# A four-layer graph network on one core: the last dense layer with features on partitions, and rooms given by what older graphs still need

## The chip, the core and the metric

The kernel runs on one core of a Trainium2 chip. Its time is the device time of one execution in microseconds (us). Before the change, three timed runs gave 2318.75, 2318.81 and 2318.9 us; the median is 2318.81.

## What is computed

There are 32 independent graphs of 512 nodes with 256 features each, and four layers; `x` is a graph's features (512 x 256) and `adj` its weights (512 x 512), all in float32. Cut to what matters, with biases kept:

```python
def L0(x):  h = (1 + eps) * x + adj @ x;      return relu(h @ W1 + b1) @ W2 + b2
def L1(x):  h = adj @ (x @ W.T + b);          return where(h > 0, h, alpha * h)
def L2(x):  h = layer_norm(x, gamma, beta)
            return x + relu((adj @ h) @ W_rel + b_rel + h @ W_root)
def L3(x):  h = (eps * x + adj @ x) @ W1 + b1               # 256 -> 1024
            h = silu(h * rsqrt(mean(h * h) + 1e-6) * w)
            return h @ W2 + b2                              # 1024 -> 256
for L in (L0, L1, L2, L3):
    x = layernorm(x + L(x))
```

The change concerns the last line of L3, `h @ W2 + b2`, and the sum with `x` that follows it.

## The kernel before

**Tiles and stages.** A graph's features are kept "by token": token 4p + c is on partition p, in chunk c, so that a tile is 128 x (4 chunks x 256 features). Between the layers' steps they are also kept with features on partitions: `aT` or `hT`, 128 x 512 tokens for each chunk of 128 features. A large product is made of seven products of blocks instead of eight (`seven`, line 651): blocks of both sides are added and subtracted beforehand (`left_sums`, `right_sums`, `weight_sums`), and the results are put together from PSUM with `take` (first write to a block) and `put` (a later one). A graph passes through `layer0`, `layer1`, `layer2`, `layer3` (lines 1046 to 1137). Each calls `aggregate` (line 767: adj @ x, 14 matmuls of 256 columns) and then its dense steps.

**Layer 3.** `layer3` (line 1100) aggregates, adds the row b2 to `x` (`plus_row`, line 1019: two additions of 128 x 512), makes the 1024 hidden features with features on partitions (`dense_feat`, line 807, into `hT`), sums their squares, takes the mean's power -1/2 through a DRAM line back to all partitions (`everywhere`, line 997: a store of `few` into `line`, then a load of `line` into a room), multiplies and applies silu, forms `right` from blocks of hidden features (`dense_sums`), and then makes the second dense layer in `dense_add` (line 850). There a block of hidden features, 128 x 128, is the stationary operand and a block of W2, 128 columns, is moved: the result is by token, and each of the seven products is added straight into `x` by VectorE. When both halves of a token half are there, `norm.half` sums the features and squares of that half for the layer norm; `norm.scaled` writes the result, and one DMA stores the graph.

**Turning.** Layer 2 needs its input turned from by-token to features on partitions. `turned` (line 973) has VectorE transpose (each 32 x 32 square by itself, two instructions of 128 x 512), and 16 moves from tile to tile then carry the squares to their partitions (`carry`, line 572: a DMA from SP's queue). In the first and the last graph (`alone`, line 515) TensorE turns instead.

**Order of the work.** Nothing is issued as it is called. `Plan.do` and `Plan.move` record operations with what they read and write; `Plan.order` (line 354) then sets an order for all engines with a table of costs (lines 32 to 90: `matmul_time`, `vector_time`, ...), earliest start first, and among those that can start at about the same time the lowest rank: graph number times a period, plus a due time counted back along the graph's own tensor work (`needs`, line 324). An operation that may go to VectorE or ScalarE (`copy`, line 551, and `Norm.put`, line 941) goes where it would end earlier. `best` tries each of `RULES` (line 95), four numbers each, and keeps the order that its own table makes shortest. All instructions are then issued in that order from one place, so nearly all have line 298 in the profile, and DMAs line 316.

**Rooms.** Buffers are not bound to stages. There are 36 rooms of 128 x 1024 in SBUF, 11 small ones, and 8 PSUM banks (lines 525 to 527), and up to five graphs in flight (line 499). A recorded tile takes a room when the first operation that touches it is put in order, and gives it back after the last. In `rooms_free` (line 380) a younger graph has to leave some rooms free: `spare` gives how many, by how far the graph is from the oldest one in flight, (0, 2, 4, 4) for rooms, (0, 1, 1) for banks.

Of the kernel before, what the change touches and what calls it, by code (L numbers as in the profile page):

```python
# [14 lines left out]
P = 128  # L15
# [76 lines left out]

RULES = [(42, 2, 10, 0.5), (42, 2, 16, 0.5)]


class Pool:

    def __init__(self, tiles, grain, spare, psum):
        self.tiles, self.grain, self.spare, self.psum = tiles, grain, spare, psum
        self.clear()

    def clear(self):
# [30 lines left out]
class Room:  # L137
# [2 lines left out]

    def __init__(self, pool, whole=True):
        self.pool, self.whole = pool, whole
        self.uses = 0
        self.clear()

# [75 lines left out]
class Plan:  # L221
# [102 lines left out]
    def needs(self, pace, near):  # L324
# [20 lines left out]
            for op, t, b in zip(self.ops, need, between)  # L345
        ]

    def best(self):


        rule = min(RULES, key=lambda rule: self.order(*rule)[0])
        return self.order(*rule)[1]

    def order(self, period, pace, last, near):

        final = max(op.graph for op in self.ops) - LATE
        rank = [
            (min(op.graph, final) * period + max(op.graph - final, 0) * last + need, i)
            for i, (op, need) in enumerate(zip(self.ops, self.needs(pace, near)))
        ]  # L360
        behind = [op.behind for op in self.ops]
        ready = [dict.fromkeys(op.ways, 0.0) for op in self.ops]
        left = {}
        for op in self.ops:
            left[op.graph] = left.get(op.graph, 0) + 1
            for r in op.rooms:
                r.clear()
                r.pool.clear()
        free = dict.fromkeys(("tensor", "vector", "scalar", "gpsimd", "sync"), 0.0)
        oldest, wire, lanes = 0, 0.0, [0.0] * LANES  # L370
        port = dict.fromkeys(free, 0.0)
        powers = {i for i, op in enumerate(self.ops) if op.port and "gpsimd" in op.ways}
        can_start = {i for i, n in enumerate(behind) if not n}
        done = []
        while can_start:
            while oldest in left and not left[oldest]:
                oldest += 1
            room_at = {}

            def rooms_free(op):  # L380

                first = [r for r in op.rooms if r.index is None]
                if not first:
                    return 0.0
                if op.graph - oldest >= self.flight:
                    return None
                at, taken = 0.0, {}
                for r in first:
                    pool = r.pool
                    if pool not in room_at:  # L390
                        room_at[pool] = pool.free()
                    whole, halves = room_at[pool]
                    k = taken.get((pool, False), 0)
                    if not r.whole and k < len(halves):
                        taken[pool, False] = k + 1
                        at = max(at, halves[k][0])
                        continue
                    n = taken.get((pool, True), 0)
                    taken[pool, True] = n + 1
                    n += pool.spare[min(op.graph - oldest, len(pool.spare) - 1)]  # L400
                    if n >= len(whole):
                        return None
                    at = max(at, whole[n][0])
                return at

            best = {}
            for i in can_start:
                op = self.ops[i]
                wait = rooms_free(op)
                if wait is None:  # L410
                    continue
                if op.kbytes and "sync" in op.ways:
                    wait = max(wait, lanes[0])
                at = {
                    e: max(free[e], wait, ready[i][e], port[e] if op.port else 0.0) for e in op.ways
                }
                way = min(
                    at, key=lambda e: at[e] + sum(op.ways[e][0]) + YIELD * (op.yields and e == "vector")
                )
                best.setdefault(way, []).append((at[way], rank[i], i))  # L420
            if not best:
                return 1e12, None
            t, engine = min((min(c)[0], e) for e, c in best.items())
            soon = t + (1e-6 if engine == "tensor" else SOON)
            _, t, i = min((r, s, i) for s, r, i in best[engine] if s <= soon)
            op = self.ops[i]
            op.start, op.way = t, engine
            busy, tail = op.ways[engine][0]
            free_before, free[engine] = free[engine], t + busy
            end = t + busy + tail  # L430
            if engine == "vector":
                idle = t - max(free_before, ready[i][engine])
                op.pause = idle if op.port and t == port[engine] else 0.0
                if op.port:
                    port["gpsimd"] = end
                if any(n in powers for n, _ in op.then):
                    port["vector"] = t + busy + PORT
            if op.kbytes:
                wire = max(wire, t + ADVANCE) + wire_time(op.kbytes)
                end = wire + op.late + AFTER  # L440
                if engine == "sync":
                    lanes = [*lanes[1:], end]
            for r in op.rooms:
                if r.index is None:
                    r.pool.take(r)
                r.left -= 1
                r.until = max(r.until, end + 0.1)
            left[op.graph] -= 1
            for n, result in op.then:
                behind[n] -= 1  # L450
                for e in ready[n]:
                    if e != engine or e != "tensor" and result:
                        ready[n][e] = max(ready[n][e], end + HAND[e])
                if not behind[n]:
                    can_start.add(n)
            can_start.remove(i)
            done.append(op)
        return max(op.start for op in done), done


@with_exitstack
def tile_gnn_stack(ctx: ExitStack, tc: tile.TileContext, a: dict, out: bass.AP):
# [53 lines left out]

        return plan.graph in (0, B - 1)

    def pool(kind, name, n, size, grain, spare):
        return Pool(  # L520
            [kind.tile([P, size], F32, tag=f"{name}{i}", name=f"{name}{i}") for i in range(n)],
            grain, spare, kind is psum,
        )

    banks = pool(psum, "ps", 8, N, N, (0, 1, 1))
    rooms = pool(work, "room", ROOMS, NC * D, P, (0, 2, 4, 4))
    smalls = pool(work, "few", SMALL, 64, 4, (0, 2, 4))


    def vector(method, n, *args, **kw):  # L530
# [319 lines left out]
    def dense_add(x, right, left, done):  # L850
# [21 lines left out]

        seven(*(bank(HC, P) for _ in range(3)), product, take, put)

    def column_sums(t):

        few = small(N // Q)
        plan.do(  # L880
            few,
            (
                "vector", "tensor_reduce", vector_time(N), (t.shaped(N // Q, Q),),
                dict(axis=mybir.AxisListType.X, op=ALU.add, apply_transpose=True),
            ),
        )
        for q in range(1, P // Q):
            add(few[0:Q], few[0:Q], few[q * Q : (q + 1) * Q])
        return few[0:Q]
# [83 lines left out]
    def turned(h):  # L973

        hT = Wide(DC)
        if alone():
            for k in range(DC):
                ps = bank(N)
                for c in range(NC):
                    flip(ps[:, c * P : (c + 1) * P], h[:, c, k * P : (k + 1) * P])  # L980
                copy(hT.chunk(k), ps)
        else:
            squares = Wide(DC)
            for k in range(DC):
                o = squares.chunk(k)
                plan.do(o, vector("transpose", N, h[:, :, k * P : (k + 1) * P]))
            places = [slice(q * Q, (q + 1) * Q) for q in range(P // Q)]
            to, of = (
                x.pair(0).then(lambda v: v.rearrange("p k (c i) -> p (k c) i", i=P))
                for x in (hT, squares)  # L990
            )
            for p in places:
                for q in places:
                    carry(to[p, :, q], of[q, :, p])
        return hT

    def everywhere(sums, ops):

# [101 lines left out]
    def layer3(x, adjacency, b):  # L1100

        aT = aggregate(x, adjacency)
        plus_row(x, b2_3)
        hT, acc = Wide(FC3), short(N)

        def squares(f):
# [17 lines left out]
        norm = (NormOnVector if alone() else Norm)(x)  # L1124
        place = out[b].rearrange("(p c) d -> p c d", c=NC)
        if b < B - 1:
            dense_add(x, right, A2_3, norm.half)
            norm.scales((1.0, LN_EPS))
            y = norm.scaled()
            plan.move(place, y, N * D / 256, into=f"out{b}")  # L1130
# [47 lines left out]
    b1_3 = col("L3_gnn_b1")  # L1178
    w_3 = col("L3_gnn_rms_weight")
    b2_3 = row("L3_gnn_b2")  # L1180
    eps3 = row("L3_gnn_epsilon")
    loop3 = constant("loop3", [P, P])
    ts(loop3, ident, eps3, None, ALU.mult)
# [52 lines left out]
```

## Time and profile before

| | |
|---|---|
| median of three runs | 2318.81 us |
| span of the profiled execution, first to last instruction | 2317.5 us |
| instructions | 41158 |
| TensorE matmul / weight load busy | 2295.5 / 2089.9 us |
| VectorE busy | 2120.0 us |
| ScalarE busy | 1642.6 us |
| GpSimd busy | 256.9 us |
| mean granted TensorE clock | 0.999 |
| DMA queue: share of 16 engines | 19.1% |

The profile is of one execution; no time apart from its span is listed for it, so that the span stands 1.3 us below the median of the timed runs. The page's first part gives each engine's busy time, its share of the span and its instructions; "PE" is a matmul, "PEld" the load of its stationary operand. The chain is the work that ended last, followed back from the last instruction. Groups of instructions are given by line, engine, operation and tiles, written "out<-in" with buffer numbers left out ("room", "ps" for a PSUM bank, "few" for a small one, "A" for sums of weight blocks, "scrap" for a result that nobody reads); then count, busy time, mean length of one in ns, and the idle time just ahead. A matmul's record is longer than the distance to the next one's start. DMA issues are listed with their size and the median time from issue to landing.

### The profile page before, as it was taken

The page shows a single profiled execution, that of the slowest core. Times are in us where ns is not written, and L with a number is a line of the kernel's source. Part 1 is how long each engine was busy: PE and PEld are TensorE (multiplying, and loading weights), DVE is VectorE, ACT ScalarE, POOL GpSimd, SP SyncE. Part 2 cuts the span into 40 slices and gives each one's busy share as a digit, 9 for nine tenths or more (in the row PEclk, how much of TensorE's full clock was granted, in tenths as well). Part 3 has the DMA queues.
Part 4 walks back from the last instruction along what each step waited for, and adds up shares of the span by engine and source line. Part 5 has one row for each costly group of instructions (what it writes and reads, how often), then busy time and mean ns, then how long its engine had stood idle before and what let it go on. Part 6 is the DMA issues. An engine that isn't in the chain of part 4 may idle for free.

```text
span 2317.5 us, 41158 instructions
## 1 busy us (share of the span) xinstructions
PE 2295.5 (99%) x14002; PEld 2089.9 (90%) x14002; DVE 2120.0 (91%) x5428; ACT 1642.6 (71%) x4444; POOL 256.9 (11%) x167
## 2 busy tenths in 40 slices
PE   9999999999999999999999999999999999999998
PEld 7889899999999999999999999999999999998988
DVE  8989999999899999999999999989999899989897
ACT  4676677776776776777767776767677677676776
POOL 0000001101101101011011111010110101101110
PEclk9999999999999999999999999999999999999999
DMA  7001222112221122211222211222112222201101
GB/s 241 21 18 19 62 58 60 24 55 62 58 60 28 54 59 65 55 43 41 56 65 57 60 25 56 61 58 59 38 46 58 65 55 52 78 13 24 55 15 42
DMA packets 223746, 122.83 MB, mean 53 GB/s; under 512 B 142896, under 2 KB 194352, under 8 KB 223536
## 3 DMA queue, kind: packets, MB, share of 16 engines
q1 hardware_dynamic: 223536, 120.20, 19.1%
q8 instruction: 111, 1.82, 0.3%
q14 instruction: 99, 0.81, 0.1%
HBM read 78.92 MB, written 24.97 MB: 45 GB/s over the span
## 4 chain that ended last, share of the span: by engine, by line
PE 89%; DVE 7%; ACT 2%; DMA 1%; issue 1%; SPq 0%; POOL 0%; ACTq 0%; DVEq 0%
PE ps L298 89%; DVE room L298 6%; ACT room L298 1%; ACT scrap L298 1%; DVE few L298 1%; DMA room<-in_x_dram 1%; DMA L_gnn_W<-in_L_gnn_W_dram 0%; DMA room<-in_adj_dram 0%; DMA L_gnn_b<-in_L_gnn_b_dram 0%; DMA diagonal<-room 0%; SPq L316 0%; ACT L298 0%; DVE A L298 0%; DVE L_gnn_W_root L298 0%; POOL few L298 0%
## 5 line engine op out<-in xcount | busy, mean ns | idle before, releaser
L298 PE MATMUL ps<-room,room 128*128 128x256 f32 x3584 | 930.9, 381 | 5.7 <-DVE room L298 3.2
L298 DVE TENSOR_TENSOR room<-room,room 128x512 f32<-128x512 f32 (+1 forms) x1360 | 773.0, 590 | 5.4 <-ACT room L298 2.8
L298 DVE TENSOR_TENSOR room<-ps,room 128x256 f32<-128x256 f32 (+1 forms) x1344 | 605.6, 469 | 143.7 <-PE ps L298 136.4
L298 PEld LDWEIGHTS ps<-room,room 128*128 128x128 f32 x3584 | 617.3, 191 | 70.3 <-DVE room L298 7.1
L298 PE MATMUL ps<-L_gnn_W,room 128*128 128x128 f32 (+1 forms) x3584 | 544.3, 290 | 1.9 <-DVE room L298 1.0
L298 PEld LDWEIGHTS ps<-L_gnn_W,room 128*128 128x128 f32 x3584 | 505.6, 191 | 33.7 <-ACT room L298 1.9
L298 PEld LDWEIGHTS ps<-A,room 128*128 128x128 f32 x3072 | 460.5, 191 | 47.3 <-DVE room L298 14.1
L298 PE MATMUL ps<-A,room 128*128 128x128 f32 x3072 | 486.9, 276 | 0.9 <-DVE room L298 0.7
L298 POOL TENSOR_TENSOR few<-few,mhalf 128x4 f32<-128x4 f32 (+2 forms) x161 | 256.2, 1598 | 2054.5 <-DVE few L298 1883.1
L298 ACT ACTIVATE room<-room,few 128x256 f32<-128x256 f32 x627 | 335.0, 596 | 159.9 <-DVE few L298 159.7
L298 PE MATMUL ps<-room,L_gnn_W 128*128 128x256 f32 x1536 | 416.4, 380 | 0.6 <-DVE room L298 0.5
L298 ACT ACTIVATE room<-ps,L_gnn_b_c 128x256 f32<-128x256 f32 x768 | 311.0, 476 | 122.3 <-PE ps L298 117.9
L298 DVE TENSOR_TENSOR room<-room 128x256 f32<-128x256 f32 (+1 forms) x640 | 308.7, 492 | 13.9 <-ACT room L298 8.2
L298 PE MATMUL ps<-room,A 128*128 128x256 f32 x1152 | 320.0, 380 | 1.1 <-ACT room L298 0.8
L298 ACT ACTIVATE room<-room 128x1024 f32<-128x1024 f32 (+2 forms) x260 | 240.8, 939 | 87.3 <-DVE room L298 84.4
L298 PEld LDWEIGHTS ps<-room,L_gnn_W 128*128 128x128 f32 x1536 | 274.5, 191 | 30.1 <-DVE room L298 1.9
L298 ACT ACTIVATE room<-ps 128x256 f32<-128x256 f32 (+1 forms) x513 | 180.1, 373 | 153.3 <-PE ps L298 153.1
L298 ACT ACTIVATE scrap<-room,few 128x256 f32<-128x256 f32 x504 | 250.7, 499 | 39.0 <-DVE few L298 38.3
L298 ACT ACTIVATE scrap<-room 128x256 f32<-128x256 f32 x504 | 206.7, 411 | 88.3 <-DVE room L298 79.8
L298 PEld LDWEIGHTS ps<-room,A 128*128 128x128 f32 x1152 | 202.8, 191 | 22.8 <-ACT room L298 2.0
L298 ACT ACTIVATE room<-room,L_gnn_rms_weight_c 128x512 f32<-128x512 f32 x256 | 173.2, 712 | 13.1 <-DVE room L298 11.0
L298 DVE TENSOR_TENSOR room<-room,loop 128x256 f32<-128x256 f32 x256 | 101.1, 411 | 2.9 <-DMA diagonal<-room 1.8
(57 smaller groups left out, 1110.6 us busy)
## 6 DMA issues: line engine op xcount, KB each, us to landing
room<-in_adj_dram SPq DMA_DIRECT2D x128, 256.0 KB, 5.0
room<-in_x_dram SPq DMA_DIRECT2D x31, 512.0 KB, 5.9
out_dram<-room SPq DMA_DIRECT2D x31, 512.0 KB, 3.2
room<-room SPq DMA_DIRECT2D x480, 32.0 KB, 2.0
diagonal<-room SPq DMA_DIRECT2D x62, 128.0 KB, 1.8
room<-in_adj_dram SPq DMA_DIRECT2D x124, 64.0 KB, 1.9
room<-diagonal SPq DMA_DIRECT2D x62, 128.0 KB, 2.2
room<-line SPq DMA_DIRECT2D x30, 256.0 KB, 3.3
```

The source lines that it names most:

```text
L298: getattr(getattr(self.nc, engine), method)(to, *(put(x) for x in args), **kw)
```

## The change

It has two parts.

In layer 3 of graphs 1 to 28 (`turn = 0 < b < B - 3`), `dense_turned` takes the place of `dense_add`: a block of W2, 128 x 128, is stationary, and the hidden features, 256 tokens, are moved, so the result has features on partitions (`yT`). ScalarE writes first results with the bias b2 added as a column (`take`), VectorE adds the later ones (`put`). VectorE then transposes `yT` in squares (two instructions), 16 moves carry the squares (`spread_squares`, taken out of `turned`), and `add_turned` adds the result to `x`. `plus_row` goes in these graphs. One more small load, `b2c_3`, brings b2 as columns.

In the planner, the fixed numbers of rooms to spare go. `safe` gives a graph a room only if each older graph in flight could still get the most that it will need at once (`peaks`), counting what the graphs before it will give back. Operations that take a room for a younger graph wait if they rank more than `AHEAD` after the first matmul that is still to be placed, unless they are due late (`LAST`). Three rules stand in `RULES` in place of two.

```diff
-RULES = [(42, 2, 10, 0.5), (42, 2, 16, 0.5)]
+RULES = [(42, 2, 10, 0.5), (44, 2, 12, 0.5), (46, 2, 10, 0.5)]
+AHEAD, LAST = 70.0, 500.0
...
+            def safe(pool, free):
+                most, slack, older = [free], 1e9, 0.0
+                for g in range(oldest, oldest + self.flight):
+                    if left.get(g):
+                        need = peaks[mine[g][reached.get(g, 0)]].get(pool, 0) + (not pool.psum)
+                        has = held.get((pool, g), 0)
+                        slack = min(slack, free + older - max(need - has, 0))
+                        older += has
+                        most.append(slack)
+                    else:
+                        most.append(most[-1])
+                return most
...
-                    n += pool.spare[min(op.graph - oldest, len(pool.spare) - 1)]
-                    if n >= len(whole):
+                    if n >= min(len(whole), most[max(op.graph - oldest, 0)]):
                         return None
...
+            front = tensor[ahead][0] + AHEAD if ahead < len(tensor) else 1e9
             for i in can_start:
                 op = self.ops[i]
+                early = op.graph > oldest and front < rank[i][0] and need[i] < LAST
+                if early and "tensor" not in op.ways and any(r.index is None for r in op.rooms):
+                    continue
...
-    banks = pool(psum, "ps", 8, N, N, (0, 1, 1))
-    rooms = pool(work, "room", ROOMS, NC * D, P, (0, 2, 4, 4))
-    smalls = pool(work, "few", SMALL, 64, 4, (0, 2, 4))
+    banks = pool(psum, "ps", 8, N, N)
+    rooms = pool(work, "room", ROOMS, NC * D, P)
+    smalls = pool(work, "few", SMALL, 64, 4)
...
+    def dense_turned(right, left, bias):
+        yT, squares, y = Wide(DC), Wide(DC), Wide(DC)
+        def product(m, ps, first):
+            n = len(right[m])
+            for k in range(n):
+                mm(ps, left[m][:, k, :], right[m][k], first and k == 0, k == n - 1)
+        def block(i, j):
+            return yT.chunk(i)[:, j * TH : (j + 1) * TH]
+        def take(ps, i, j):
+            act(block(i, j), ps, AF.Identity, bias=bias[:, i : i + 1])
+        def put(ps, i, j, more):
+            if more:
+                add(block(i, j), ps, block(i, j))
+            else:
+                take(ps, i, j)
+        seven(*(bank(TH) for _ in range(3)), product, take, put)
+        for k in range(DC):
+            plan.do(squares.chunk(k), vector("transpose", N, yT.chunk(k)))
+        spread_squares(y, squares)
+        return y.pair(0).then(lambda v: v.rearrange("p k (c i) -> p c k i", i=P))
+    def add_turned(x, y, done):
+        x = x.then(lambda v: v.rearrange("p c (k i) -> p c k i", i=P))
+        for h in range(2):
+            add(half(x, h), half(x, h), half(y, h))
+            done(h)
...
         aT = aggregate(x, adjacency)
-        plus_row(x, b2_3)
+        turn = 0 < b < B - 3
+        if not turn:
+            plus_row(x, b2_3)
...
-            dense_add(x, right, A2_3, norm.half)
+            if turn:
+                add_turned(x, dense_turned(right, A2_3, b2c_3), norm.half)
+            else:
+                dense_add(x, right, A2_3, norm.half)
...
+    b2c_3 = col("L3_gnn_b2")
```

More of the change, by code (lines that the diff above doesn't have):

```diff
@@ L90, with __init__ @@
 LATE = 3
-RULES = [(42, 2, 10, 0.5), (42, 2, 16, 0.5)]
+RULES = [(42, 2, 10, 0.5), (44, 2, 12, 0.5), (46, 2, 10, 0.5)]
+AHEAD, LAST = 70.0, 500.0
 class Pool:
-    def __init__(self, tiles, grain, spare, psum):
-        self.tiles, self.grain, self.spare, self.psum = tiles, grain, spare, psum
+    def __init__(self, tiles, grain, psum):
+        self.tiles, self.grain, self.psum = tiles, grain, psum
         self.clear()
@@ L142, in __init__ @@
         self.pool, self.whole = pool, whole
+        self.size = 1.0 if whole else 0.5
         self.uses = 0
@@ L346, in needs, with peaks @@
         ]
+    def peaks(self):
+        first, last = {}, {}
+        for i, op in enumerate(self.ops):
+            for r in op.rooms:
+                first.setdefault(r, i)
+                last[r] = i
+        use, held = [], {}
+        for i, op in enumerate(self.ops):
+            for r in op.rooms:
+                if first[r] == i:
+                    k = r.pool, op.graph
+                    held[k] = held.get(k, 0) + r.size
+            use.append({r.pool: held[r.pool, op.graph] for r in op.rooms})
+            for r in op.rooms:
+                if last[r] == i:
+                    held[r.pool, op.graph] -= r.size
+        most, peaks = {}, [None] * len(self.ops)
+        for i in range(len(self.ops) - 1, -1, -1):
+            g = self.ops[i].graph
+            now = dict(most.get(g, {}))
+            for pool, n in use[i].items():
+                now[pool] = max(now.get(pool, 0), n)
+            most[g] = peaks[i] = now
+        return peaks
     def best(self):
@@ L356, in order @@
         final = max(op.graph for op in self.ops) - LATE
+        need = self.needs(pace, near)
         rank = [
-            (min(op.graph, final) * period + max(op.graph - final, 0) * last + need, i)
-            for i, (op, need) in enumerate(zip(self.ops, self.needs(pace, near)))
+            (min(op.graph, final) * period + max(op.graph - final, 0) * last + n, i)
+            for i, (op, n) in enumerate(zip(self.ops, need))
         ]
+        tensor = sorted(r for r, op in zip(rank, self.ops) if "tensor" in op.ways)
         behind = [op.behind for op in self.ops]
@@ L369, in order @@
         free = dict.fromkeys(("tensor", "vector", "scalar", "gpsimd", "sync"), 0.0)
-        oldest, wire, lanes = 0, 0.0, [0.0] * LANES
+        oldest, ahead, wire, lanes = 0, 0, 0.0, [0.0] * LANES
+        peaks, held, mine, reached = self.peaks(), {}, {}, {}
+        for i, op in enumerate(self.ops):
+            mine.setdefault(op.graph, []).append(i)
+        finished = [False] * len(self.ops)
         port = dict.fromkeys(free, 0.0)
@@ L390, in rooms_free @@
                     if pool not in room_at:
-                        room_at[pool] = pool.free()
-                    whole, halves = room_at[pool]
+                        whole, halves = pool.free()
+                        room_at[pool] = whole, halves, safe(pool, len(whole))
+                    whole, halves, most = room_at[pool]
                     k = taken.get((pool, False), 0)
@@ L404, in rooms_free @@
                 return at
+            while ahead < len(tensor) and finished[tensor[ahead][1]]:
+                ahead += 1
+            front = tensor[ahead][0] + AHEAD if ahead < len(tensor) else 1e9
             best = {}
@@ L443, in order @@
             for r in op.rooms:
+                k = r.pool, op.graph
                 if r.index is None:
                     r.pool.take(r)
+                    held[k] = held.get(k, 0) + r.size
                 r.left -= 1
                 r.until = max(r.until, end + 0.1)
+                if not r.left:
+                    held[k] -= r.size
             left[op.graph] -= 1
@@ L457, in order @@
             done.append(op)
+            finished[i] = True
+            n, my = reached.get(op.graph, 0), mine[op.graph]
+            while n < len(my) - 1 and finished[my[n]]:
+                n += 1
+            reached[op.graph] = n
         return max(op.start for op in done), done
@@ L517, in alone, with pool @@
         return plan.graph in (0, B - 1)
-    def pool(kind, name, n, size, grain, spare):
+    def pool(kind, name, n, size, grain):
         return Pool(
             [kind.tile([P, size], F32, tag=f"{name}{i}", name=f"{name}{i}") for i in range(n)],
-            grain, spare, kind is psum,
+            grain, kind is psum,
         )
-    banks = pool(psum, "ps", 8, N, N, (0, 1, 1))
-    rooms = pool(work, "room", ROOMS, NC * D, P, (0, 2, 4, 4))
-    smalls = pool(work, "few", SMALL, 64, 4, (0, 2, 4))
+    banks = pool(psum, "ps", 8, N, N)
+    rooms = pool(work, "room", ROOMS, NC * D, P)
+    smalls = pool(work, "few", SMALL, 64, 4)
     def vector(method, n, *args, **kw):
@@ L986, in turned, with spread_squares @@
                 plan.do(o, vector("transpose", N, h[:, :, k * P : (k + 1) * P]))
[L987 to L994, printed above, removed]
-        return hT
+            spread_squares(hT, squares)
+        return hT
+    def spread_squares(to, of):
+        places = [slice(q * Q, (q + 1) * Q) for q in range(P // Q)]
+        to, of = (
+            x.pair(0).then(lambda v: v.rearrange("p k (c i) -> p (k c) i", i=P))
+            for x in (to, of)
+        )
+        for p in places:
+            for q in places:
+                carry(to[p, :, q], of[q, :, p])
     def everywhere(sums, ops):
```

## The prediction

> **What bounds the kernel now.** I read busy shares first, then the chain of work that ended last, the busy table by stretch, the timeline of single rows, the groups of instructions by form, the waits, and the DMA issues. Busy shares and chain:
>
> ```profile
> PE 2295.5 (99%) x14002; PEld 2089.9 (90%) x14002; DVE 2120.0 (91%) x5428; ACT 1642.6 (71%) x4444; POOL 256.9 (11%) x167
> ...
> PE 89%; DVE 7%; ACT 2%; DMA 1%; issue 1%; SPq 0%; POOL 0%; ACTq 0%; DVEq 0%
> ```
>
> TensorE (PE) is busy nearly always, and 89% of the chain is its matmuls. VectorE (DVE) at 91% is the next bound. By stretch (columns: PE, weight load, DVE, ACT, POOL busy, each with its count, then clock, DMA share, GB/s):
>
> ```profile
> 400.00:2000.00 1600.00, 1599.82 (x9795) 1462.00 (x9794) 1469.41 (x3729) 1154.94 (x3144) 186.39 (x113) 1.00 0.20 53
> ```
>
> Over 1600 us in the middle PE is without a gap. One graph passes in 71.18 us: the load of a diagonal, issued once a graph, starts at 1016.08, 1087.26 and 1158.44 in SP's timeline. Per graph DVE is busy 1469.41/1600 x 71.18 = 65.4 us, ACT 51.4. So the middle counts in matmul time. Single rows of PE (start, length, count; "x14" is 14 records; a matmul leaves two, 14002 for the 7013 that the program holds):
>
> ```profile
> 2202.51 3.18 PE L298 MATMUL ps<-L_gnn_W,room 128*128 128x256 f32 x14
> 2205.53 0.59 PE L298 MATMUL ps<-room,room 128*128 128x256 f32 x2
> ```
>
> ```profile
> 2275.64 1.72 PE L298 MATMUL ps<-L_gnn_W,room 128*128 128x128 f32 x14
> 2277.20 0.39 PE L298 MATMUL ps<-A,room 128*128 128x128 f32 x2
> ```
>
> What counts is the distance between starts, not the 381 or 275 ns length of a record, since records overlap. 256 columns: 3.02/14 = 0.216 us a record; over the unmixed run from 2186.10 to 2214.16, 130 records, 0.2158. 128 columns: 1.56/14 = 0.111; over the run from 2275.64 to 2290.37, 132 records, 0.1116. So a matmul of 256 columns takes 0.4317 us and one of 128 columns 0.2232: twice the columns, 1.934 times the time.
>
> [...]spacings give 2270 us of work (6810 x 0.2159 + 7192 x 0.1112) where 2295.5 is shown busy. [...]
>
> **The change part by part.** Rows of single durations (groups by form, and DMA issues):
>
> ```profile
> L298 PE MATMUL ps<-A,room 128*128 128x128 f32 x3072 | 486.9, 276 | 0.9 <-DVE room L298 0.7
> ...
> L298 DVE TENSOR_TENSOR room<-ps,room 128x256 f32<-128x256 f32 x1056 | 419.1, 410 | 74.6 <-PE ps L298 70.8
> ...
> L298 ACT ACTIVATE room<-ps,L_gnn_b_c 128x256 f32<-128x256 f32 x768 | 311.0, 476 | 122.3 <-PE ps L298 117.9
> ...
> L298 DVE TENSOR_TENSOR room<-room,L_gnn_b 128x512 f32<-128x512 f32 x128 | 87.1, 682 | 0.7 <-PE ps L298 0.6
> ...
> L298 DVE STREAM_TRANSPOSE room<-room 128x512 f32<-128x512 f32 x60 | 41.9, 703 | 0.7
> ```
>
> ```profile
> room<-room SPq DMA_DIRECT2D x480, 32.0 KB, 2.0
> ```
>
> *TensorE, on the path.* In the 28 turned graphs (1 to 28) `dense_add` of layer 3 goes: 7 products x 4 chunks x 2 = 56 matmuls of 128 columns, 56 x 0.2232 = 12.50 us. In comes `dense_turned`: 7 x 4 = 28 of 256 columns, 28 x 0.4317 = 12.09. Saved: 0.41 us a graph, 28 x 0.41 = 11.5 us. The lower end: [...]with spacings averaged over the whole trace (0.1112 and 0.2163), 12.45 - 12.11 = 0.34, 9.5 us. I take 10.5, between the two trace values. The order in which the built program's instructions stand agrees: 218 PE instructions a graph become 190, the same sequence each period, and the planner keeps rule (42, 2, 10, 0.5).
>
> *VectorE, beside.* Out: 2 row additions (2 x 0.682) and 7 additions from PSUM (7 x 0.410), 4.23 us. In: 3 from PSUM (1.23), 2 transposes (1.41), 2 additions of 512 elements, 1.37, priced at the 682 ns row. Their pieces of 128 with a swapped order have no row; bounded by 0.67 each as a plain addition and two 256-element ones, 0.82, so at most 0.3 us more a graph. The planner also moves 3 of 4 scalings of the last norm from ACT to DVE (3 x 0.407 by the row of that form, 1.22). Net +1.0 us: 66.4 of a period of 70.8, 94%. This costs nothing while 4.4 us a graph stay free; where DVE stands late just ahead of a matmul, it costs up to that 1.0.
>
> *ScalarE, beside.* In: 4 activations with a bias from PSUM, 4 x 0.476 = 1.90; out: 3 x 0.596. Net +0.1 on 51.4. Banks are then freed by ACT, whose 20 us of idle time a graph cover it.
>
> *Moves.* 16 more a graph on SP, 0.609 us each to issue (median of such issues): 9.7 us. SP's timeline shows it issuing nothing from 1111.8 to 1126.1 and from 1138.2 to 1158.4 of one period, so they fit. In the new order seven stand ahead of a restore and of graph g+1's line store (the RMS factor's way to all partitions), two and one between, six behind its read: 7 x 0.61 = 4.3 us can delay that line. DMA share 0.20 grows by 28 x 16 x 256 packets x 13 ns / 16 engines = 93 us, 4 points. All of it lies behind other graphs' matmuls, since in a turned graph nothing of TensorE follows `dense_turned`. The chain transposes, moves, landing, addition (1.4 + 9.7 + 2.0 + 0.7 = 14 us) only keeps x and two more rooms busy longer. `add_turned` now waits for a DMA: behind it on DVE stand other graphs' additions, which matmuls await. The planner's own 3.6 us per move (issue to landing) against the 2.0 measured makes me put it at 0; an added wait can't gain, and if it isn't covered it costs up to 1 us a graph.
>
> *Rooms, orders.* The new rule for rooms moves no work in the middle, whose PE was full. It reorders the ends: two matmuls of graph 3 no longer stand at PE place 93 to 98. Stalls (spacing beyond 0.2159/0.1112) sum to 17 us before 200 us, 7 us after 2000, and 0.4 a graph between. Nothing there has a row for the new order: -5 to +5 us, I take 0. The bias column load is one 1 KB DMA, 0.
>
> *Sum.* 2317.5 - 10.5 = 2307.0 of span; the runs' median 2318.8 lies 1.3 above the span, so 2308.3.
>
> **Rivals.** (a) *VectorE takes over what TensorE gives back.* For: 94% busy, 3 more scalings, and the 0.4 us of stalls a graph are all waits for DVE. Against: 4.4 us free. Half to all of the 10.5 is lost by 0.2 to 0.4 us of new stalls a graph: 2313.5 to 2319, I say 2316.5. (b) *SP's line store stuck behind the seven moves, or `add_turned` ahead of its landing, holds DVE in order* in each turned graph. For: 4.3 us of issues ahead of a line whose reader is DVE; the line load alone lands in 3.3 us. Against: the moves now on SP show waits of 0.3 us in all. It is slower by over 0.2% from (10.5 + 4.6)/28 = 0.54 us uncovered a graph; at 0.75, 28 x 0.75 = 21: 2318.8 + 21 - 10.5 = 2329. (c) *The ends gain too*: of the stalls before 200 us and after 2000, 24 us, a third goes, since the rule for rooms now keeps room for old graphs: 2308.3 - 8 = 2300. For: each of those stalls is a wait for DVE or ACT, which also serve younger graphs there. Against: no row shows that rooms cause them. (d) *The change doesn't act*: the order shows it does; no chance given.
>
> **How the numbers follow.** Chances: forecast (2303 to 2314.2) 0.62; (c) 0.12; (a) 0.15; (b) 0.11. A measurement of this kernel can tell about 0.2%, 4.6 us, from none: 2314.2 to 2323.4 is "same". Faster 0.62 + 0.12 + about 0.02 of (a) = 0.76; same 0.14; slower 0.10. The range takes in most of (c) and of (a): 2299.5 to 2319.
>
> **What would show it.** In the profile after: x1568 more matmul records of 256 columns and 3136 fewer of 128; a period of 70.8 us instead of 71.18; PE still without a gap from 400 to 2000; DVE about 93 to 94%. Wrong if the period stays at 71.2 (then new PE waits for DVE of 0.2 us and more a graph: rival a), if it grows and DVE waits for `room<-room` or `room<-line` (rival b), or if the middle is as said and the ends aren't.

## The result, and the profile after

The changed kernel takes 2325.57 us (median of 9 runs, 2324.5 to 2330.11); the kernel before, beside it, 2319.14 (9 runs). The ratio is 1.003, interval 1.002 to 1.0039: slower by 0.3%, where 0.45% faster was forecast. The profiled execution spans 2327.3 us against 2317.5; it is the slowest of the nine (2330.11 us).

Busy shares and the chain of work that ended last, after:

```profile
PE 2294.8 (99%) x12434; PEld 2034.1 (87%) x12434; DVE 2155.1 (93%) x5502; ACT 1642.0 (71%) x4478; POOL 239.5 (10%) x167
...
PE 72%; DVE 21%; ACT 2%; issue 2%; DMA 2%; SPq 0%; DVEq 0%; POOLq 0%; POOL 0%; ACTq 0%
```

There are 1568 fewer matmul records, and yet TensorE's busy time is the same (2294.8 us, 2295.5 before). VectorE's share of the chain has gone from 7% to 21%. The busy table by stretch, and then the waits of weight loads and matmuls from 400 to 2000 us, after:

```profile
400.00:2000.00 1600.00, 1594.69 (x8523) 1409.49 (x8522) 1496.77 (x3803) 1146.08 (x3139) 170.07 (x112) 1.00 0.25 61
```

```profile
PEld ps L303 <- DVE room L303: 23.6, 64, 1.0
PEld ps L303 <- issue: 8.3, 33, 0.3
PEld ps L303 <- ACT room L303: 4.7, 23, 0.2
...
PE ps L303 <- DVE room L303: 3.6, 12, 0.6
```

In the kernel before, weight loads waited less for VectorE in this stretch, and no matmul waited for it:

```profile
PEld ps L298 <- DVE room L298: 11.4, 44, 0.3
```

The prediction named a sign of being wrong: a period that stays at 71.2 us. It came true. The stores of a diagonal in SP's timeline after start 71.24 us apart, where 70.8 was forecast:

```profile
1055.95 2.84 SPq L321 DMA_DIRECT2D diagonal<-room  x2
...
1127.19 2.85 SPq L321 DMA_DIRECT2D diagonal<-room  x2
```

A piece of the chain after, in order of time, shows how it comes about (start, length, what):

```profile
1149.85 17.19 PE ps L303 x79
...
1171.60 4.76 DVE room L303 x12
1176.40 49.36 PE ps L303 x280
1225.79 4.12 DVE room L303 x8
1229.98 2.47 DVE room L303 x4
```

TensorE's row stops at a matmul whose operand is the last of a dozen VectorE instructions in a row; in VectorE's own timeline no idle time stands ahead of any of them. The matmuls there:

```profile
1175.20 1.06 PE L303 MATMUL ps<-room,A 128*128 128x256 f32 x4
1176.40 0.70 PE L303 MATMUL ps<-room,L_gnn_W 128*128 128x256 f32 x2
```

Four records of 256 columns, at the spacing of 0.216 us that the trace has elsewhere (median), take 0.864 us, so the next should start at 1176.06. It starts 0.34 us later. The records show no more than 0.14 us of that as idle time, as a record is longer than the spacing (0.38 us here).

**A measure of stalls that records can't hide.** I sum, over all matmul records, the distance to the next start less 0.2159 us (256 columns) or 0.1112 us (128). "Work" is the sum of those unit times, so it is a count of matmuls at the spacings of the kernel before and not a measurement of its own; "tail" is the time from the end of the last matmul to the end of the span. Matmuls at a lower granted clock count as stalls too. All in us, from the profiled execution of each kernel; times are medians, ratios are to the kernel before in runs beside it.

| kernel | time | ratio, interval | work | stalls before 400 / 400 to 2000 / later | tail |
|---|---|---|---|---|---|
| before | 2319.14 | | 2269.9 | 18.8 / 11.8 / 7.0 | 8.6 |
| after | 2325.57 | 1.003, 1.002 to 1.0039 | 2259.7 | 22.8 / 23.8 / 7.1 | 12.6 |
| mm_only | 2351.1 | 1.0133, 1.0119 to 1.0147 | 2259.7 | 19.4 / 44.7 / 15.9 | 8.2 |
| mm_frozen | 2321.59 | 1.0009, 1.0003 to 1.0016 | 2259.7 | 22.0 / 22.0 / 8.4 | 8.6 |
| rooms_only | 2327.3 | 1.003, 1.0018 to 1.0041 | 2269.9 | 23.3 / 17.7 / 8.8 | 7.9 |
| turn_only | 2340.68 | 1.0088, 1.0075 to 1.0102 | 2259.7 | 19.4 / 30.7 / 20.8 | 7.0 |
| scale_act | 2362.24 | 1.0181, 1.0167 to 1.0195 | 2259.7 | 21.5 / 53.9 / 11.3 | 12.6 |
| no_moves | 2324.95 | 1.0022, 1.0014 to 1.0031 | 2259.7 | 20.5 / 22.2 / 7.0 | 12.6 |
| vec_less | 2299.55 | 0.9911, 0.9897 to 0.9924 | 2259.7 | 14.4 / 2.5 / 6.3 | 12.6 |
| before_less | 2305.55 | 0.9939, 0.9925 to 0.9952 | 2269.9 | 14.4 / 2.3 / 6.4 | 8.6 |
| rooms_less | 2305.73 | 0.994, 0.9927 to 0.9952 | 2269.9 | 14.0 / 3.0 / 7.6 | 7.9 |
| mm_less | 2300.09 | 0.9914, 0.99 to 0.9927 | 2259.7 | 16.3 / 5.0 / 7.3 | 8.6 |
| table | 2302.88 | 0.9924, 0.991 to 0.9938 | 2259.7 | 13.2 / 10.3 / 4.7 | 13.7 |
| before_table | 2318.74 | 0.9999, 0.999 to 1.0007 | 2269.9 | 15.3 / 18.6 / 1.9 | 11.3 |
| rooms_table | 2304.25 | 0.9936, 0.9924 to 0.9949 | 2269.9 | 12.6 / 2.6 / 6.4 | 9.9 |
| turn_table | 2315.92 | 0.9983, 0.9977 to 0.999 | 2259.7 | 19.2 / 11.9 / 13.6 | 7.9 |
| table_split | 2311.74 | 0.9967, 0.9954 to 0.9979 | 2269.9 | 13.2 / 6.8 / 4.6 | 13.7 |
| two_adds | 2297.91 | 0.9906, 0.9892 to 0.9919 | 2259.7 | 17.5 / 1.6 / 3.8 | 11.8 |
| adds_no_turn | 2307.16 | 0.9944, 0.9931 to 0.9956 | 2269.9 | 13.3 / 4.9 / 4.1 | 10.6 |
| before_adds | 2343.06 | 1.0096, 1.008 to 1.0111 | 2269.9 | 21.2 / 31.7 / 9.6 | 7.6 |

So the profiled executions differ by -10.2 (work) + 4.0 + 12.0 + 0.1 (stalls) + 4.0 (tail) = +9.9 us; their spans by +9.8. Most of the +4.0 before 400 us is the clock in this one execution: its granted clock was 0.50 from 102.92 to 109.75 us, where 14 matmul records of 256 columns are spaced by about 0.43 us and lose 3.1 us in sum. The execution before has 1.00 there, and of two others in the changed kernel's order, no_moves has such a stretch half as long and vec_less none. Without these 3.1 us the spans differ by 6.7 us, near the medians' 6.4. The tail is ScalarE's: its timeline after has graph 30's last scalings between the sums of graph 31, and the last pair starts at 2322.66, 7.9 us after the last matmul's end (2314.8). Before, the last four started 2.6 us after it.

### The profile page after: what moved, and what is told of

The parts are those of the page before. It is cut to its first block, busy times and chain, and to the rows that moved or that the text cites. A ratio compares the mean times of both kernels' runs of the same rounds, so it can differ in the third digit from the quotient of the medians.

```text
span 2327.3 us, 38580 instructions
## 1 busy us (share of the span) xinstructions
PE 2294.8 (99%) x12434; PEld 2034.1 (87%) x12434; DVE 2155.1 (93%) x5502; ACT 1642.0 (71%) x4478; POOL 239.5 (10%) x167
## 4 chain that ended last, share of the span: by engine, by line
PE 72%; DVE 21%; ACT 2%; issue 2%; DMA 2%; SPq 0%; DVEq 0%; POOLq 0%; POOL 0%; ACTq 0%
PE ps L303 72%; DVE room L303 18%; DVE few L303 3%; ACT room L303 2%; DMA room<-line 1%; ACT scrap L303 0%; SPq L321 0%; DMA room<-in_x_dram 0%; DMA room<-room 0%; DMA diagonal<-room 0%; DVE pause L1313 0%; DVE A L303 0%; DVEq L303 0%; DVE L_gnn_W L303 0%; ACT L303 0%
## 5 line engine op out<-in xcount | busy, mean ns | idle before, releaser
L303 PE MATMUL ps<-room,L_gnn_W 128*128 128x256 f32 x2432 | 650.1, 382 | 6.4 <-DVE room L303 4.6
L303 PEld LDWEIGHTS ps<-room,L_gnn_W 128*128 128x128 f32 x2432 | 448.5, 190 | 74.9 <-DVE room L303 20.1
L303 PE MATMUL ps<-room,A 128*128 128x256 f32 x1824 | 485.4, 380 | 1.5 <-DVE room L303 1.2
L303 POOL TENSOR_TENSOR few<-few,mhalf 128x4 f32<-128x4 f32 (+3 forms) x161 | 238.8, 1484 | 2082.2 <-DVE few L303 1731.9
L303 ACT ACTIVATE room<-ps,L_gnn_b_c 128x256 f32<-128x256 f32 x880 | 356.1, 478 | 82.1 <-PE ps L303 80.4
L303 PEld LDWEIGHTS ps<-room,A 128*128 128x128 f32 x1824 | 342.7, 190 | 51.0 <-issue 1.8
L303 PE MATMUL ps<-L_gnn_W,room 128*128 128x128 f32 (+1 forms) x1792 | 340.4, 305 | 1.4 <-DVE room L303 1.4
L303 PEld LDWEIGHTS ps<-L_gnn_W,room 128*128 128x128 f32 x1792 | 285.7, 191 | 26.7 <-DVE room L303 2.2
L303 PEld LDWEIGHTS ps<-A,room 128*128 128x128 f32 x1728 | 238.4, 191 | 20.9 <-DVE room L303 9.6
L303 PE MATMUL ps<-A,room 128*128 128x128 f32 x1728 | 253.4, 276 | 2.6 <-DVE room L303 2.6
```

The source lines that it names most:

```text
L303: getattr(getattr(self.nc, engine), method)(to, *(put(x) for x in args), **kw)
```

## The experiments

Where an order is "kept", the plan is made as in the kernel named, and only what is issued at a place changes. Otherwise the planner orders everything anew.

**Theories.** *VectorE*: its late results hold TensorE. *Rooms*: the new rule itself makes a worse order. *Moves*: SP's queue or landings hold VectorE. *Price*: the wide matmul isn't worth 10 us.

**1. mm_only: wide matmuls, nothing else, planned again.**

```diff
+            if wide:
+                for k in range(n):
+                    flat = ps.then(lambda v: v.rearrange("p c i -> p (c i)"))
+                    mm(flat, left[m][:, k, :], right[m][k], first and k == 0, k == n - 1)
+                return
...
-            dense_add(x, right, A2_3, norm.half)
+            dense_add(x, right, A2_3, norm.half, wide=0 < b < B - 3)
```

The products land in `x` in the wrong layout; turning and its sums are left out.

> The kernel before, with one thing changed: in graphs 1 to 28 the second dense layer of layer 3 is made by 28 matmuls of 256 columns in place of 56 of 128, and the products are added into x as they come, in the wrong layout (turning and its sums are left out, so the output of these graphs is not the reference's). If matmuls were priced right, it takes 2319.1 - 10.5 = 2308.6 us (2307 to 2311); if the wide matmul is not worth it, 2317 to 2321. All theories of the lost gain (VectorE, moves, room rule) expect the first.

Measured 2351.1, a miss of 40 us. By count TensorE has 10.2 us less work, but the new order has 80.0 us of stalls in place of 37.6. All theories had missed this: an order planned anew can by itself be worth tens of us, as run 2 confirms.

**2. mm_frozen: the same, in the order of before.**

```diff
+                if wide:
+                    flat = ps.then(lambda v: v.rearrange("p c i -> p (c i)"))
+                    def issue(flat=flat, w=left[m][:, k, :], r=right[m][k], start=first and k == 0, stop=k == n - 1):
+                        nc.tensor.matmul(
+                            flat.place(), w, r.place(), start=start, stop=stop, skip_group_check=True
+                        )
+                    one, two = plan.ops[-2:]
+                    one.ways = {"tensor": (one.ways["tensor"][0], lambda: None)}
+                    two.ways = {"tensor": (two.ways["tensor"][0], issue)}
```

> The kernel before in its own order, each pair of narrow matmuls of layer 3's second dense layer in graphs 1 to 28 issued as one of 256 columns at the place of the second (products land in x in the wrong layout; turning is left out). Nothing else moves. If the wide matmul is worth what was priced, 2319.5 - 10.5 = 2309 us (2306 to 2312), and the loss in mm_only was the new order's. If the shorter TensorE work is eaten by VectorE at once, 2316 to 2321.

Measured 2321.59. With nothing moved, 10.2 us less of TensorE work bring nothing (the time is 0.1% longer), and stalls rise from 37.6 to 52.4. So TensorE alone didn't set the pace in the order of before.

**3. rooms_only: the planner's whole new part (room rule, `AHEAD`, three rules to choose from), no graph turned.**

```diff
-        turn = 0 < b < B - 3
+        turn = False
```

> The changed kernel with no graph turned: only the planner's new rule for rooms. If the room rule and its order lose the gain, 2324 us or more. If VectorE's added work or the moves lose it, as before within 2: 2317 to 2321.

Measured 2327.3: the planner's part costs 8 us, as much as the whole change, with none of the turned layer's sums or moves in it. Here "rooms" was right. The runs spread from 2325.47 to 2330.85; the three with a mean granted clock of 0.999 took under 2326, so 6 of the 8 us stand without a lower clock.

**4. turn_only: the turned layer under the old rule.** The diff is the change's planner part undone, `spare` with it.

> The turned dense layer with the planner of before (fixed rooms to spare). If VectorE's or the moves' added work loses the gain, it stays at 2322 to 2330 us. If the room rule loses it, 2307 to 2313.

Measured 2340.68, beyond both ranges. So the rule for rooms isn't the only loss: the turned layer under the old rule costs 21 us.

**5. scale_act: the three scalings back on ScalarE, order kept.**

```diff
+            if turn:
+                on_scalar.update(id(op) for op in plan.ops[first:] if len(op.ways) == 2)
...
-            op.ways[op.way][1]()
+            op.ways["scalar" if id(op) in on_scalar else op.way][1]()
```

> The changed kernel, its order kept, with the three scalings a graph that went to VectorE put on ScalarE at the same place in the order. If VectorE's load is what TensorE waits for, its 1.2 us less a graph give back most of the 0.4 us of new stalls a graph: 28 x 0.4 = 11, 2313 to 2318 us. If moves or rooms are the cause, unchanged: 2324 to 2328.

Measured 2362.24, far from either. From 400 to 2000 us VectorE was busy for less time (1447.25 us, 1496.77 in the changed kernel), but there it now waited 36.8 us for ScalarE's rooms where it had waited 6.5, and TensorE more for VectorE:

```profile
PEld ps L303 <- DVE room L303: 59.9, 126, 1.1
...
DVE room L303 <- ACT room L303: 36.8, 44, 1.4
PE ps L303 <- DVE room L303: 24.7, 52, 0.7
```

Three scalings are 1.5 us on ScalarE (in the changed kernel, the three that start at 2317.00 take 1.47 us to the next start), in front of results that VectorE waits for. That doesn't refute "VectorE"; it shows that 1.5 us a graph more on ScalarE, in this place, goes through to TensorE although ScalarE is busy for only 1162.16 of these 1600 us.

**6. no_moves: the 16 added moves left out, order kept.**

```diff
+        first = len(plan.ops)
         spread_squares(y, squares)
+        skipped.update(id(op) for op in plan.ops[first:])
...
-            op.ways[op.way][1]()
+            if id(op) not in skipped:
+                op.ways[op.way][1]()
```

> The changed kernel in its own order with the 16 added moves a graph left out (the turned result is then added from a stale buffer, so output is not the reference's). If SP's queue or late landings hold VectorE, 2313 to 2318 us; if not, 2323 to 2327.

Measured 2324.95, within the scatter of the changed kernel. "Moves" falls.

**7. vec_less: six small additions a graph left out, order kept.** `column_sums` sums over partitions: a reduction, then three additions that bring four groups of 32 partitions onto one. A graph has it twice, for the row sums of its weights (layer 1) and for the squares of the hidden features (layer 3). The rows of VectorE in the changed kernel led here (start, length):

```profile
1131.11 0.72 DVE L303 TENSOR_TENSOR room<-ps,room 128x256 f32<-128x256 f32 x2
1131.86 0.16 DVE L303 TENSOR_TENSOR few<-few 32x16 f32<-32x16 f32 x1
1132.06 0.69 DVE L303 TENSOR_TENSOR room<-room,room 128x512 f32<-128x512 f32 x1
1132.76 0.16 DVE L303 TENSOR_TENSOR few<-few 32x16 f32<-32x16 f32 x1
1132.96 0.43 DVE L303 TENSOR_TENSOR room<-room,loop 128x256 f32<-128x256 f32 x1
1133.40 0.17 DVE L303 TENSOR_TENSOR few<-few 32x16 f32<-32x16 f32 x1
1133.60 0.43 DVE L303 TENSOR_TENSOR room<-room,loop 128x256 f32<-128x256 f32 x1
1133.94 0.42 DVE L303 TENSOR_TENSOR room<-ps,room 128x256 f32<-128x256 f32 x1
```

The addition with `loop` at 1132.96 has a small addition behind it and takes 0.44 us to the next start; the same operation at 1133.60, with none behind it, takes 0.34. The small one takes 0.20 itself. A small addition thus costs 0.30 us, where the planner's table (`vector_time(16)`) has 0.077.

```diff
             add(few[0:Q], few[0:Q], few[q * Q : (q + 1) * Q])
+            if 0 < plan.graph < B - 3:
+                skipped.add(id(plan.ops[-1]))
...
-            op.ways[op.way][1]()
+            if id(op) not in skipped:
+                op.ways[op.way][1]()
```

> The changed kernel in its own order with the six small VectorE additions a graph of column_sums left out in graphs 1 to 28 (row sums and square sums are then incomplete). The trace has each at 0.2 us where the planner's table has 0.077, and the wide instruction ahead lengthened by 0.1. If VectorE running behind its plan stalls TensorE, 28 x 0.4 = 11 us or more come back: 2308 to 2316. If not, 2323 to 2327.

Measured 2299.55: 26.0 us less, twice what was expected. From 400 to 2000 us the stalls fall from 23.8 to 2.5. The waits and the chain of vec_less in that stretch:

```profile
PEld ps L303 <- DVE room L303: 1.6, 2, 1.3
PEld ps L303 <- ACT room L303: 0.6, 3, 0.2
```

```profile
176.68 1765.78 PE ps L303 x9554
1960.30 70.29 PE ps L303 x390
```

Now the chain doesn't leave TensorE's row for 1765.78 us. That alone proves little, as it didn't in the kernel before for nearly as long, though 11.8 us of stalls lie between 400 and 2000 us:

```profile
277.72 1688.78 PE ps L298 x10329
```

The sums of spacings tell more: an estimated 28 x 6 x 0.30 = 50 us of VectorE's time went, and 30.4 us of TensorE's stalls with it (3.1 of them the clock's), in an order that is otherwise the same. A rival: three of the six stand in the way of the RMS factor, so that leaving them out also shortens that path. But VectorE waited for the factor's load only 1.3 us in the changed kernel's whole trace, which shows no other engine waiting for it. "VectorE" is shown.

**8. before_less, 9. rooms_less, 10. mm_less: the same six left out of the kernel before, of rooms_only and of mm_frozen, orders kept.** The edit is that of vec_less.

> The kernel before in its own order without the six small VectorE additions a graph of column_sums in graphs 1 to 28 (sums incomplete). If VectorE already set the pace in the kernel before, its 0.4 us of stalls a graph go: 2319 - 11 = 2308 us (2304 to 2311). If the kernel before was bound by TensorE alone, 2316 to 2319.

> The new rule for rooms with no graph turned, in its own order, without the same small additions. If its 8 us over the kernel before are VectorE running late in that order, they go with the stalls: 2301 to 2311 us. If the order itself is bad (rooms, moves, ScalarE), 2318 to 2327.

> mm_frozen (order of before, 28 wide matmuls in place of 56 narrow ones, turning left out) without the same small additions. If VectorE alone kept the wide matmuls' saving from the end, this is 10 us under before_less: 2296 to 2301 us. If the saving is worth less than priced, 2304 or more.

Measured 2305.55, 2305.73 and 2300.09. The kernel before loses 14.7 us (2320.28 beside it): VectorE held it too, 14.5 us of its 37.6 us of stalls. So with the six additions the change costs 6.4 us, and without them, in the same two orders, it gains 6.0 (2299.55 against 2305.55): VectorE's lateness turned the sign. rooms_only loses 21.6 us and then equals before_less, and weight loads' waits for VectorE from 400 to 2000 us go from 13.0 us to 0.8, so most of the rule's 8 us were VectorE running late in that order, not a lack of rooms. mm_less is 5.5 us under before_less: half the price of the wide matmuls comes through in this order, and the stalls keep the rest (28.7 against 23.1). Weight loads wait there for ScalarE (5.9 us from 400 to 2000 us) and still for VectorE (4.2).

**11. table: the changed kernel planned with VectorE's costs as the trace has them.**

```diff
+def turn_time(n):
+    return 0.628, 0.085
+def few_time(n):
+    return 0.3, 0.085
...
-            add(few[0:Q], few[0:Q], few[q * Q : (q + 1) * Q])
+            way = "vector", "tensor_add", few_time(16), (few[0:Q], few[q * Q : (q + 1) * Q]), {}
+            plan.do(few[0:Q], way)
```

Transposes and the transposing reduction get `turn_time`, a piece of `by_token` 0.17 us.

> The changed kernel planned again with VectorE's costs as the trace has them: 0.3 us for a small addition of column_sums with what it adds to its neighbours, 0.17 for a piece of by_token, 0.628 for a transpose. If the plan's error on VectorE loses the gain, 2308 to 2316 us. If any new order differs by chance, it may lie anywhere from 2312 to 2345.

Measured 2302.88, 22.7 us under the changed kernel and better than either range, with nothing left out (the planner again chooses between VectorE and ScalarE for some operations). Planned with four costs corrected at once, the same work holds TensorE less: stalls fall from 53.6 to 28.2 us. Which of the four mattered wasn't tried.

**12. before_table, 13. rooms_table, 14. turn_table: the same costs without both parts of the change, without the turned layer, without the room rule.** The edits are those of 11 on the kernel before, on 3 and on 4.

> The kernel before (no graph turned, rooms to spare fixed) planned with VectorE's costs as the trace has them, as in table. If the corrected costs alone made table fast, it gains as much: 2303 to 2309 us. If VectorE is full in either case and the order of before already suits it, 2314 to 2322.

> The new rule for rooms with no graph turned, planned with the corrected costs. If the turned layer is worth its 10.5 us once the plan knows VectorE's time, 10 us over table: 2311 to 2316. If the turned layer is worth nothing even then, 2301 to 2306.

> The turned layer with the rooms to spare of before and the corrected costs. If the new rule for rooms has no part in table's time, 2301 to 2307 us. If it is needed, 2312 or more.

Measured 2318.74, 2304.25 and 2315.92. Right costs alone do nothing; together with the new rule for rooms they give 14.9 us, and the turned layer adds 1.4 to that. The expectation that the turned layer would be worth 10 us here was a miss.

**15. table_split: table in its own order, each wide matmul issued as two of 128 columns.**

```diff
+                def issue(w=left[m][:, k, :], r=right[m][k], start=first and k == 0, stop=k == n - 1):
+                    o, r = ps.place(), r.place()
+                    for c in range(2):
+                        at = slice(c * P, (c + 1) * P)
+                        nc.tensor.matmul(
+                            o[:, at], w, r[:, at], start=start and c == 0, stop=stop, skip_group_check=True
+                        )
```

> The kernel table in its own order, each wide matmul of the turned layer issued as two of 128 columns. If the wide matmul's saving reaches the end once VectorE is not late, 28 x 0.37 = 10 us more: 2311 to 2315. If VectorE still sets the pace, 2302 to 2305.

Measured 2311.74, 8.9 us more. "Price" falls: in an order where VectorE is less late, nearly all of the saving reaches the end.

**16. two_adds: table, with two small additions in place of three.**

```diff
-        for q in range(1, P // Q):
-            way = "vector", "tensor_add", few_time(16), (few[0:Q], few[q * Q : (q + 1) * Q]), {}
-            plan.do(few[0:Q], way)
+        for n in (2 * Q, Q):
+            way = "vector", "tensor_add", few_time(16), (few[0:n], few[n : 2 * n]), {}
+            plan.do(few[0:n], way)
```

> table with the three small additions of column_sums made two (64 partitions onto 64, then 32 onto 32), planned again; nothing left out. VectorE has about 2 x 0.3 = 0.6 us a graph less: if it still sets the pace in table, up to 28 x 0.37 = 10 us less, 2293 to 2300 us; if table's order is free of VectorE's stalls, 2300 to 2305.

Measured 2297.91, the fastest kernel here that leaves nothing out: 0.94% under the kernel before. In the middle its stalls are 1.6 us, and nearly all waits for VectorE are gone:

```profile
PEld ps L311 <- ACT scrap L311: 1.9, 11, 0.3
PEld ps L311 <- DVE room L311: 0.3, 1, 0.3
```

**17. adds_no_turn: two_adds with no graph turned (the edit of 3).**

> two_adds with no graph turned, planned again. If the turned layer pays once VectorE is not late, TensorE's 10 us come back: 2304 to 2309 us against 2298. If it pays nothing, 2295 to 2300.

Measured 2307.16, so the turned layer is worth 9.3 us in this setting, where both orders were planned anew.

**18. before_adds: the kernel before with two additions in place of three, planned again with its old costs.**

> The kernel before with two small additions in place of three in column_sums, everything else kept, planned again with its old costs. If VectorE's late small additions are what holds TensorE, about a third of before_less's 14.7 us, 2311 to 2316 us; if the new order undoes it, 2318 to 2325.

Measured 2343.06, beyond both ranges: less work and 24 us slower. The same two additions stand in two_adds, the fastest kernel, so it is the order again.

## Why the prediction was wrong

**What bounds the kernel: wrong.** The prediction read 1599.82 us of 1600 as "PE is without a gap" and counted the middle in matmul time. It had itself computed 0.4 us of stalls a graph from spacings, and set them aside. Those were 11.8 us in the middle, 0.5 a graph, and before_less shows that VectorE caused 9.5 of them. In the kernel before both engines paced it together.

**TensorE's term: right in size.** Counted with the prediction's own spacings it is 10.2 us, against 10.5 taken; the measurements are table_split (8.9 us) and adds_no_turn (9.3 us), where nearly all of it reaches the end. In mm_frozen none does.

**VectorE's term: the step that failed.** "This costs nothing while 4.4 us a graph stay free." The busy time was sized right (1496.77 of 1600 us, 94% as said), but its free 6% isn't there when a result is due: in the piece shown, twelve VectorE instructions stand in a row ahead of the matmul that waits. The prediction bounded the cost at the 1.0 us a graph that the change adds; it didn't ask what VectorE already cost. Part of VectorE's added time was not in its sum: the kernel issues small writes to a tile `pause` on VectorE where the plan has it idle, 85 of them (8.3 us) in the middle after, 22 (2.2 us) before. No run leaves them out, so what they cost is open. Rival (a), put at 0.15 and 2316.5 us, named the mechanism, with too small a price: the middle's new stalls are 12.0 us, 0.5 a period.

**Rooms and orders: the second step that failed.** "The new rule for rooms moves no work in the middle, whose PE was full", taken as 0. rooms_only puts it at +8 us, and rooms_less shows how: in the new order VectorE holds TensorE more. The -5 to +5 us kept for the ends could not hold that. At the ends the profiled execution has 4.0 us more of tail and, apart from the clock, 0.9 us more at the start.

**Moves and ScalarE's added work.** no_moves confirms the 0 for moves; rival (b), "slower", ended on the right side by luck, as its way (moves ahead of the line's store) isn't what happened. What ScalarE's banks cost wasn't tried by itself.

**What decides the sum.** The two parts aren't additive: rule +8, turned layer +21 under the old rule, both together +6; with the right costs the rule is worth -14.5 against before_table, the turned layer -1.4 or, with two_adds' shorter sums, -9.3. Why a given order suits VectorE's true times is only partly explained. Right costs for VectorE take 22.7 us off the changed kernel, 23.1 off rooms_only and 24.8 off turn_only, each in a new order; yet before_table, with the same costs and the old rule, still has 18.6 us of stalls in the middle, and before_adds 31.7. What in these two orders makes VectorE late is open.

## What to carry to other kernels

TensorE's row looked full because records of 381 ns stood 216 ns apart, so that a stall of up to 0.16 us left no gap in it: sum the distances between starts before calling an engine full, and ask of the next engine not how much of it is free but whether it is free just ahead of the work that waits. When an order is planned from a table of costs, a change moves the order too; test it with the order kept, and mend the table with durations between starts, small instructions first.

## What the runs showed of the hardware

In the changed kernel's trace a VectorE addition of 32 x 16 elements cost 0.30 us of that engine, 0.20 itself and 0.10 on the instruction ahead, though its record is 0.16 us. In the rows shown with vec_less the addition ahead, a record of 0.43 us, is followed 0.44 us after its start instead of 0.34, and the small addition that follows carries no wait of its own. Over the whole trace, where neither follower carries a wait, the medians are 0.44 us (43 times) against 0.34 (726) behind an addition of 128 x 256, and 0.71 (38) against 0.60 (219) behind one of 128 x 512. What causes these 0.10 us was not shown. Of the 0.20 us behind the small addition, half goes with a wait: 179 of 192 followers carry a wait on the semaphore that VectorE itself raises and start 0.20 us after it (median); the 13 that don't, start 0.10 us after it.
